# Products behind attention outputs as four products of 32 columns, one kind of PSUM bank, early identity products and another order of work, in a kernel of two transformer blocks

## The chip, the cores and the metric

The kernel runs on one core of a Trainium2 chip. The metric is the device time of one execution in microseconds, the median of several runs. "PE" is TensorE's matmul side, "PEld" its weight loads, DVE is VectorE, ACT ScalarE, POOL GpSimd, SP the engine that issues the DMAs.

## The reference

Two transformer blocks are applied to x, of 32 sequences with 128 positions and 256 features, all in fp32. Each block has self attention (16 heads of 16 features), cross attention to a context of 32 x 128 x 256, and a feed-forward layer of 1024. Both are conditioned by a vector for each sequence. Cut to what matters:

```python
# first block
mod = silu(t_emb) @ ada_w + ada_b              # six parts: shift, scale, gate for two places
xm1 = ln(x) * (1 + scale_sa) + shift_sa
q, k, v = split(xm1 @ qkv_w + qkv_b)
x = x + gate_sa * (softmax(q k^T * SCALE) v @ sa_proj_w + sa_proj_b)
qc = ln(x) @ q_w + q_b ; kc, vc = split(context @ kv_w + kv_b)
x = x + softmax(masked(qc kc^T * SCALE)) vc @ ca_proj_w + ca_proj_b
h = gelu((ln(x) * (1 + scale_ff) + shift_ff) @ fc1_w + fc1_b)
x = x + gate_ff * (h @ fc2_w + fc2_b)
# second block: the same stages, rotary embedding of q and k, adaptive layer norms before
# each stage, no gates and no biases in attention
```

## The kernel before

The 32 sequences are taken in 16 groups of two (256 columns). Each group passes through both blocks, and eight groups ("streams") are under way at a time. A stage of a stream is a Python generator. It yields when its next step could run (a time, an engine, the buffers it needs, a rank), and `Tasks.run` (L143) always steps the task that could start first on its engine. The instructions are issued in this order, and every engine executes its own in order.

The times by which it chooses are a planner's: `Clock` (L41) holds for each engine when it will be free, with costs written by hand (`clock.use("pe", 0.86 * n)`), an addition of `TURN` where PE's way of dividing its array changes ("full", "rows", "columns"), and a time for each buffer. `ORDER` (L35) holds a number for each 40 us of planned time; it changes the ranks and the patience of the choice in that stretch, and so the order of the work. None of these numbers exists at run time; only the order does.

PE divides its array in three ways. *Full*: the projections with 128 x 128 weights and 256 columns of data, that is `rows_T` (L590, products transposed to features x positions, at L598), `values` (L603, at L610) and `project` (L813, at L836), and the transposes against the identity (L559 for normalized y, L748 for the attention maxima). *Rows*: scores, 16 products of 32 rows a batch, four beside each other (`group_rows` L720, at L723). *Columns*: attention outputs, 16 products of 32 columns a batch (L769), four beside each other.

An attention batch takes: first scores (L732), the maxima by VectorE (L735, two reductions), the maxima turned by PE (L748), subtraction from the queries (L752), second scores (L757), exp by ScalarE (L761, two of them), outputs with the sums of the exponentials (L769), a copy to `ou` (L775). When both batches of a group are copied, `over_sums` (L780) sends the sums through DMAs: `few`, reciprocal, `inv` in DRAM, and back spread out as `ou`, multiplied into `xt` (L803). `project` multiplies xt by the output weights.

PSUM has eight banks: `scores` takes four (one buffer), `small` one (turned maxima and outputs, L236), `products` three (everything else, L237). A piece of PE's work takes a free one with `clock.take` and another engine's step gives it back.

At the start SP issues loads in this order: rows (L284), embT (L287), cols (L290), ada_w's first part into the place of w_fc1 (L313), x of group 0 (L317), w_qkv. PE's first products are the modulations (L448, ada_w by the silu of the condition).

Of the kernel before, what the change touches and what calls it, by code (L numbers as in the profile page):

```python
# [17 lines left out]
P = 128  # L18
# [3 lines left out]
GB = 2  # L22
# [12 lines left out]
ORDER = (  # L35
    200, 7, 0, 0, 0, 0, 297, 0, 0, 0, 0, 0, 0, 0, 0, 0, 129, 264, 0, 0, 0, 312, 0, 0, 0, 388, 0, 0, 109, 188, 182,
    0, 0, 0, 292, 58
)


class Clock:  # L41
# [3 lines left out]
    HOP, DRAIN, TABLE, PACE = 0.06, 0.22, 1.28, 1.03  # L45
    TURN = {"full": 0.15, "rows": 0.1, "columns": 0.1}

    def __init__(self):
        self.free = dict.fromkeys(("pe", "dve", "act", "pool", "sp", "none"), 0.0)
        many = {"sc": 1, "at": 1, "mm": 3, "pt": 2, "set": NA, "qa": 2, "ou": 3, "st": 2, "ht": 1,  # L50
                "y": 3, "cx": 3, "x": NS + 1}
        self.slots = {kind: [0.0] * n for kind, n in many.items()}
        self.table, self.way = None, "full"
        self.now = 0.0
        self.landed = 2.0

    def use(self, engine, took, way="full"):

        if engine in ("exp", "gelu"):
            if engine != self.table:  # L60
                took += self.TABLE
                self.table = engine
            engine = "act"
        if engine == "pe":
            took = took * self.PACE + (self.TURN[way] if way != self.way else 0.0)
            self.way = way
        self.free[engine] = max(self.now, self.free[engine]) + took
        return self.free[engine] + (self.DRAIN if engine == "pe" else self.HOP)
# [154 lines left out]
def two_blocks(ctx: ExitStack, tc: tile.TileContext, a: dict, out: bass.AP):  # L223
# [11 lines left out]
    scs = [psum.tile([P, R, C * S], F32, name="scores")]  # L235
    ats = [psum.tile([P, C * S], F32, name="small")]  # L236
    mms = [psum.tile([P, 2 * GT], F32, name=f"products{i}") for i in range(3)]  # L237
    streams = [Stream(const, i) for i in range(NS)]
# [9 lines left out]
    p_a = pool("p_a", 1)  # L248
    p_s = pool("p_s", NS + 2)

    def mm(shape):
# [10 lines left out]
    def weight(rows, cols, uses, *names):  # L262

        t = const.tile([P, rows // P, cols], F32, name=f"w_{names[0]}")

        def second():
            n = cols // len(names)
            for i, name in enumerate(names):
                load(t[:, :, i * n:(i + 1) * n], f"L1_xcond_{name}")
                end = clock.dma(6.0)  # L270
            return end

        return Weight(t, uses, second)
# [7 lines left out]
    w_fc2 = weight(DF, D, 1, "ffn_w2")  # L281

    rows = const.tile([P, C + 2], F32, name="rows")
    nc.sync.dma_start(out=rows, in_=a["rows"])  # L284

    embT = {name: const.tile([P, KC, B], F32, name=f"embT_{name}") for name in ("raw", "silu")}
    nc.sync.dma_start(out=embT["raw"], in_=a["cond_1024"])  # L287

    cols = const.tile([P, a["vectors"].shape[1]], F32, name="cols")
    nc.sync.dma_start(out=cols, in_=a["vectors"])  # L290
    for _ in range(3):
        clock.load(32)
# [12 lines left out]


    ada_lo, late = w_fc1.t, w_fc2.t.rearrange("p (k n) d -> p k (n d)", k=KC)
    ada_hi = late[:, :, 0:2 * D]
    lnw = [late[:, :, 2 * D:], ada_lo[:, :, 0:2 * D], ada_hi]
    spare = [t.rearrange("p f n -> p (f n)") for t in ht]  # L310
    clock.slots["ht"] = [NEVER]
    src = a["L0_xcond_ada_w"].rearrange("(c p) n -> p c n", p=P)
    nc.sync.dma_start(out=ada_lo[:, :, 0:2 * D], in_=src[:, :, 0:2 * D])  # L313
    t_ada = clock.load(512)

    def load_x(t, src, g):
        nc.sync.dma_start(out=t, in_=src[g * GB:(g + 1) * GB].rearrange("b s d -> s b d"))  # L317

    def load_ctx(i, g):
        nc.sync.dma_start(out=cxs[i], in_=a["ctx_1024"].rearrange("(c p) n -> p c n", p=P)[:, :, g * GT:(g + 1) * GT])  # L320

    load_x(xs[0], a["x"], 0)
    t_x0 = clock.load(256)
    load(w_qkv.t, "L0_xcond_qkv_w")
    w_qkv.there[0] = clock.load(768)

    ident = const.tile([P, P], F32, name="ident")
    make_identity(nc, ident)
    neg_half = const.tile([P, GB], F32, name="neg_half")
    nc.gpsimd.memset(neg_half, -0.5)  # L330
# [130 lines left out]
    def the_first():  # L461
        t = max(t_ada, 6.5)
        scale = yield from modulation(t, 0, "sa_scale", ada_lo, "silu", c_ada, D, D, True)
        shift = yield from modulation(t, 0, "sa_shift", ada_lo, "silu", c_ada, 0, 0, False)
        mods["L0", "sa"] = scale, shift
# [124 lines left out]
    def rows_T(w, col, src, n):  # L590
# [4 lines left out]
        for c in range(n):  # L595
            for k in range(KC):
                at = col + c * P
                nc.tensor.matmul(ps[:, c, :], lhsT=w.t[:, k, at:at + P], rhs=src[:, k, :],  # L598
                                 start=(k == 0), stop=(k == KC - 1))
        w.used()  # L600
        return slot, ps, clock.use("pe", 0.86 * n)

    def values(wm, hd, w, col, src, t):  # L603
# [4 lines left out]
        for b in range(GB):  # L608
            for k in range(KC):
                nc.tensor.matmul(ps[:, b, :], lhsT=src[:, k, b * S:(b + 1) * S],  # L610
                                 rhs=w.t[:, k, col:col + D], start=(k == 0), stop=(k == KC - 1))
        w.used()
        t = clock.use("pe", 1.72)
        there = Event()
# [49 lines left out]
    def plain(to, wm, w, src, t, bias):  # L664
# [6 lines left out]
        def move():  # L671
# [6 lines left out]
            for e in range(2):  # L678
                nc.sync.dma_start(out=to[0:P:2, e:C:2, :], in_=st[64 * e:64 * e + 64, 0:KC, :])
                end = clock.dma(2.4)  # L680
            clock.give("st", at, there.add(end))
# [4 lines left out]
    def turned(to, wm, w, col, src, t):  # L686
# [7 lines left out]
        def move():  # L694
# [10 lines left out]
            for e in range(2):  # L705
                nc.sync.dma_start(out=to[2 * e:P:4, :, :], in_=st[:, 0, e, :])
                end = clock.dma(2.4)
            clock.give("st", at, there.add(end))
# [4 lines left out]
    def attention(wm, hd, masked, t, t_v, name, done):  # L713
# [13 lines left out]
        def batch(b):  # L727
# [14 lines left out]
            clock.give("sc", slot, t_top)  # L742
            yield (lambda: max(t_top, when(second[b - 1]) if b else 0.0)), "pe", "at qa" if ou else "at qa ou", 0.5
            at, less = clock.take("at"), clock.take("qa")
            if not ou:
                ou.append(clock.take("ou"))
            ps = ats[at][:, 0:S]
            nc.tensor.transpose(ps, top.rearrange("p r i -> p (r i)"), ident)  # L748
# [4 lines left out]
            end = clock.use("dve", 0.7)  # L753
            clock.give("at", at, end)
            yield end, "pe", "sc pt", 0
# [7 lines left out]
            clock.give("sc", slot, end)  # L763
            yield (lambda: max(end, when(t_v))), "pe", "at", 1
            at = clock.take("at")
            for c in range(C):
                for r in range(R):
                    i = (R * c + r) * HD
                    nc.tensor.matmul(ats[at][32 * r:32 * r + 32, c * S:(c + 1) * S],  # L769
                                     lhsT=v[:, b, i:i + HD, :].rearrange("p d t -> p (d t)"),  # L770
# [3 lines left out]
            yield end, "act", "", 1  # L774
            nc.scalar.copy(ous[ou[0]][:, :, cut], ats[at].rearrange("p (c s) -> p c s", s=S))  # L775
            end = clock.use("act", 0.6)
            clock.give("at", at, end)
            copied.add(end)

        def over_sums():  # L780
# [6 lines left out]
            nc.sync.dma_start(out=few, in_=o[1:P:8, :, :])  # L787
            at = clock.dma(2.2)
            nc.sync.dma_start(out=wm.xt, in_=o[0:P:2, :, :])
            clock.dma(2.0)  # L790
            yield at, "dve", "", 1
# [3 lines left out]
            nc.sync.dma_start(out=inv.rearrange("r (t w) -> (r t) w", w=w), in_=few)  # L795
            yield clock.dma(1.7), "sp", "", 1
            by = o[:, 0:KC, :]
            for c in range(2):
                half = inv[:, c * KC * GT:(c + 1) * KC * GT]
                nc.sync.dma_start(out=by[c:P:2, :, :], in_=half.unsqueeze(1).to_broadcast([n, 4, KC * GT]))  # L800
                at = clock.dma(2.2)
            yield at, "dve", "", 1.5
# [10 lines left out]
    def project(wm, x, lhs, n, w, ready, bias, gate, name):  # L813


        if bias is not None:
            bias = biases[bias]
        if gate is not None:
            y, gate = gate, ys[gate]
        if bias is not None:  # L820
            for b in range(GB):
                if gate is None:
                    nc.gpsimd.tensor_tensor(x[:, b, :], x[:, b, :], bias, ALU.add)
                else:
                    gb = p_s.tile([P, D], F32, tag="gb", name=f"gb_{name}_{b}", bufs=2)
                    nc.gpsimd.tensor_tensor(gb, gate[:, b, :], bias, ALU.mult)
                    nc.gpsimd.tensor_tensor(x[:, b, :], x[:, b, :], gb, ALU.add)
                    clock.use("pool", 0.7)
                clock.use("pool", 0.7)
        for b in range(GB):  # L830
# [4 lines left out]
            for k in range(n):  # L835
                nc.tensor.matmul(ps[:, b, :], lhsT=lhs(k, b), rhs=w.t[:, k, :], start=(k == 0), stop=(k == n - 1))  # L836
            t = clock.use("pe", 0.43 * n)
        w.used()
# [55 lines left out]
    class Context:  # L894
# [5 lines left out]
        def fetch(self, wm):  # L900
# [3 lines left out]
            load_ctx(self.slot, self.g)  # L904
            self.there.add(clock.dma(3.3))

# [68 lines left out]
    def stream(wm, mine, loaded):  # L975

        while loaded:
# [13 lines left out]
            def next_x(i):  # L991
                load_x(xs[i], a["x"] if then < NG else middle, then % NG)
                return xs[i], clock.dma(3.3)

# [113 lines left out]
```

## Time and profile before

| what | value |
|---|---|
| median of 6 runs | 1481.52 us (1479.39 to 1486.67) |
| the profiled execution's own time | 1482.65 us |
| its span, first to last instruction | 1480.5 us |
| mean granted TensorE clock | 0.995 |
| PE busy, records | 1438.1 us (97%), 16992 |
| L598 on w_ffn_w, 1024 records of 128 x 256 | 238.5 us busy, mean 384 ns |
| L769 outputs, 4096 records of 128 x 128 | 138.6 us busy, mean 276 ns |
| L735 reductions of scores, 256 | 299.9 us busy, mean 1213 ns |
| L761 exp, 256 | 248.3 us busy, mean 1022 ns |
| DMA | 120.49 MB, 25.5% of 16 engines |

[...] In a timeline line the columns are the start, the length from the first start to the last end, engine, line, operation, what is written and read, the part of the array (rows*columns), the data's shape and the number of records. In brackets stands an idle time before it and what ended it. In the list of waits a line says who waited for whom: us in total, times, longest.

### The profile page before, as it was taken

The page shows a single profiled execution, that of the slowest core. Times are in us where ns is not written, and L with a number is a line of the kernel's source. Part 1 is how long each engine was busy: PE and PEld are TensorE (multiplying, and loading weights), DVE is VectorE, ACT ScalarE, POOL GpSimd, SP SyncE. Part 2 cuts the span into 40 slices and gives each one's busy share as a digit, 9 for nine tenths or more (in the row PEclk, how much of TensorE's full clock was granted, in tenths as well). Part 3 has the DMA queues.
Part 4 walks back from the last instruction along what each step waited for, and adds up shares of the span by engine and source line. Part 5 has one row for each costly group of instructions (what it writes and reads, how often), then busy time and mean ns, then how long its engine had stood idle before and what let it go on. Part 6 is the DMA issues. An engine that isn't in the chain of part 4 may idle for free.

```text
span 1480.5 us, 39505 instructions
## 1 busy us (share of the span) xinstructions
PE 1438.1 (97%) x16992; PEld 1184.1 (80%) x16992; DVE 876.5 (59%) x1514; ACT 711.7 (48%) x1150; POOL 360.3 (24%) x498
## 2 busy tenths in 40 slices
PE   7999999999999999999999999999999999999998
PEld 6787878788888887887787887888788787888887
DVE  7665555555555555557468565667487656656531
ACT  6544545445555554544444534544444443544452
POOL 3031323321232322333223231222032121202110
PEclk9999999999999999999999999999999999999999
DMA  6333223222223133233223241221223111211201
GB/s 220 123 98 91 70 61 101 69 80 84 65 78 102 57 93 97 67 94 99 68 82 105 73 140 64 65 79 55 80 83 115 64 56 57 80 41 65 73 26 40
DMA packets 107358, 120.49 MB, mean 81 GB/s; under 512 B 11632, under 2 KB 82992, under 8 KB 107184
## 3 DMA queue, kind: packets, MB, share of 16 engines
q1 hardware_dynamic: 107184, 117.98, 25.5%
q8 instruction: 133, 2.18, 0.6%
q14 instruction: 41, 0.34, 0.1%
HBM read 54.92 MB, written 12.68 MB: 46 GB/s over the span
## 4 chain that ended last, share of the span: by engine, by line
PE 79%; DMA 7%; DVE 7%; issue 2%; SPq 2%; ACT 2%; POOL 1%; DVEq 0%; ACTq 0%; POOLq 0%
PE products L598 25%; PE products L836 21%; PE scores L723 15%; PE small L769 7%; PE products L610 6%; PE products L559 3%; DVE top L735 2%; PE small L748 1%; DMA ou<-inv_a 1%; ACT exp L761 1%; DVE y L547 1%; DVE xt L803 1%; DMA ou<-inv_b 1%; DMA ou<-inv_e 1%; DMA inv_b<-few_b 1%
## 5 line engine op out<-in xcount | busy, mean ns | idle before, releaser
L761 ACT ACTIVATE exp<-scores 128x1024 f32<-128x1024 f32 x256 | 248.3, 1022 | 169.8 <-PE scores L723 160.0
L735 DVE TENSOR_REDUCE top<-scores 128x8 f32<-128x1024 f32 x256 | 299.9, 1213 | 45.1 <-PE scores L723 44.6
L598 PE MATMUL products<-xt,w_ffn_w 128*128 128x256 f32 x1024 | 238.5, 384 | 0.4 <-ACT ht L865 0.4
L836 PE MATMUL products<-w_ffn_w,ht 128*128 128x256 f32 x1024 | 232.6, 382 | 0.0
L598 PEld LDWEIGHTS products<-xt,w_ffn_w 128*128 128x128 f32 x1024 | 189.5, 190 | 31.9 <-issue 3.4
L836 PEld LDWEIGHTS products<-w_ffn_w,ht 128*128 128x128 f32 x1024 | 191.8, 190 | 28.1 <-issue 1.2
L723 PEld LDWEIGHTS scores<-qa,keys 32*128 32x128 f32 x4096 | 126.7, 187 | 51.0 <-issue 24.7
L775 ACT COPY ou<-small 128x512 f32<-128x512 f32 x128 | 75.6, 590 | 189.2 <-PE small L769 187.5
L865 ACT ACTIVATE ht<-products,cols 128x256 f32<-128x256 f32 x256 | 116.2, 474 | 104.6 <-PE products L598 103.7
L723 PE MATMUL scores<-qa,keys 32*128 32x128 f32 x4096 | 151.1, 284 | 9.1 <-ACT exp L761 3.5
L723 PEld LDWEIGHTS scores<-keys,queries 32*128 32x128 f32 x4096 | 126.0, 186 | 37.3 <-issue 22.9
L723 PE MATMUL scores<-keys,queries 32*128 32x128 f32 x4096 | 150.5, 283 | 3.3 <-ACT exp L761 1.5
L769 PE MATMUL small<-exp,values 128*32 128x128 f32 x4096 | 138.6, 276 | 2.5 <-DVE qa L752 2.4
L703 POOL TENSOR_TENSOR st<-st 128x512 f32<-128x512 f32 x64 | 83.8, 1312 | 230.0 <-DVE st L698 208.9
L841 DVE TENSOR_TENSOR x<-products,x 128x512 f32<-128x512 f32 x64 | 44.1, 688 | 139.9 <-PE products L836 139.2
L752 DVE TENSOR_TENSOR qa<-queries,small 128x512 f32<-128x512 f32 x128 | 86.9, 679 | 67.4 <-PE small L748 64.7
L598 PE MATMUL products<-xt,w_qkv_w 128*128 128x256 f32 x512 | 125.8, 392 | 0.8 <-DVE xt L579 0.8
L769 PEld LDWEIGHTS small<-exp,values 128*32 128x32 f32 x4096 | 104.2, 110 | 25.4 <-issue 11.5
L598 PEld LDWEIGHTS products<-xt,w_qkv_w 128*128 128x128 f32 x512 | 96.5, 196 | 16.5 <-issue 2.0
L803 DVE TENSOR_TENSOR xt<-xt,ou 128x512 f32<-128x512 f32 x64 | 47.8, 747 | 84.9 <-DMA ou<-inv_b 26.6
L698 DVE TENSOR_TENSOR st<-products,rope 128x512 f32<-128x512 f32 x128 | 81.5, 682 | 13.8 <-PE products L598 9.6
L845 DVE TENSOR_TENSOR y<-products,y 128x512 f32<-128x512 f32 x32 | 22.1, 690 | 109.3 <-PE products L836 93.4
(109 smaller groups left out, 1758.7 us busy)
## 6 DMA issues: line engine op xcount, KB each, us to landing
xt<-ou SPq DMA_DIRECT2D x64, 256.0 KB
keys<-st SPq DMA_DIRECT2D x96, 128.0 KB
queries<-st SPq DMA_DIRECT2D x96, 128.0 KB
cxt<-in_ctx SPq DMA_DIRECT2D x32, 256.0 KB
x<-in_x SPq DMA_DIRECT2D x16, 256.0 KB
keys<-st SPq DMA_DIRECT2D x16, 256.0 KB
y<-gate_dram_sa SPq DMA_DIRECT2D x16, 256.0 KB
ou<-inv_a SPq DMA_DIRECT2D x32, 128.0 KB
```

The source lines that it names most:

```text
L598: nc.tensor.matmul(ps[:, c, :], lhsT=w.t[:, k, at:at + P], rhs=src[:, k, :], start=(k == 0), stop=(k == KC - 1))
L610: nc.tensor.matmul(ps[:, b, :], lhsT=src[:, k, b * S:(b + 1) * S], rhs=w.t[:, k, col:col + D], start=(k == 0), stop=(k == KC - 1))
L698: nc.vector.tensor_tensor(st[:, :, :, one], ps[:, :, one].unsqueeze(2).to_broadcast([P, 2, 2, S]), rope, ALU.mult)
L703: nc.gpsimd.tensor_tensor(st[:, 0], st[:, 0], st[:, 1], ALU.add)
L723: nc.tensor.matmul(sc[:, r, c * S:(c + 1) * S], lhsT=lhs(slice(32 * r, 32 * r + 32), c), rhs=rhs(slice(32 * r, 32 * r + 32), c), start=Tru ...
L735: nc.vector.tensor_reduce(top[:, r:r + 2, TOP:TOP + 2 * C:2], scs[slot][:, r:r + 2, :].rearrange("p r (c s) -> p r c s", s=S), AX.X, ALU.max)
L752: nc.vector.tensor_tensor(qa, q[:, :, cut], ps.unsqueeze(1).to_broadcast([P, C, S]), ALU.subtract)
L761: nc.scalar.activation(exps[pt][r // 2], scs[slot][:, r:r + 2, :], AF.Exp, scale=SCALE)
L769: nc.tensor.matmul(ats[at][32 * r:32 * r + 32, c * S:(c + 1) * S], lhsT=v[:, b, i:i + HD, :].rearrange("p d t -> p (d t)"), rhs=exps[pt][r ...
L775: nc.scalar.copy(ous[ou[0]][:, :, cut], ats[at].rearrange("p (c s) -> p c s", s=S))
L836: nc.tensor.matmul(ps[:, b, :], lhsT=lhs(k, b), rhs=w.t[:, k, :], start=(k == 0), stop=(k == n - 1))
L865: nc.scalar.activation(ht[f // (FC // 2)][:, f % (FC // 2), :], ps[:, 0, :], AF.Gelu, bias=b1[:, f:f + 1])
```

## The change

Five things change:

- `multiply` replaces the plain matmul in `rows_T`, `values` and `project`. If the planner's state of PE is "columns" when the product is issued, it is issued as four products of 32 of its output rows each; otherwise as before. The planner's way "any" stays in columns if PE is there and is full otherwise. `TURN` is now charged for the way that is left.
- `small` is gone. There are four `products` banks, and turned maxima and outputs take one of these too.
- At the start embT and ada_w are loaded first, then rows, x of group 0 and cols. Twelve products of the identity with itself are issued on PE as soon as the identity is made; nothing reads them.
- `project` waits in the planner until its bias row exists.
- Some planned costs (DMA times, the time of the first modulation) and the numbers in `ORDER` are others. The order of the work differs throughout.

```diff
 ORDER = (
-    200, 7, 0, 0, 0, 0, 297, 0, 0, 0, 0, 0, 0, 0, 0, 0, 129, 264, 0, 0, 0, 312, 0, 0, 0, 388, 0, 0, 109, 188, 182,
-    0, 0, 0, 292, 58
+    76461, 23488, 0, 0, 0, 11198, 21064, 0, 0, 70525, 0, 0, 82594, 39864, 78145, 0, 87173, 36332, 67761, 88325, 0,
+    384, 0, 49384, 42794, 64772, 95724, 36861, 38189, 70264, 536, 60140, 7381, 59045, 89734, 0, 0
 )
...
-    TURN = {"full": 0.15, "rows": 0.1, "columns": 0.1}
+    TURN = {"full": 0.1, "rows": 0.15, "columns": 0.15}
...
-        many = {"sc": 1, "at": 1, "mm": 3, "pt": 2, "set": NA, "qa": 2, "ou": 3, "st": 2, "ht": 1,
+        many = {"sc": 1, "mm": 4, "pt": 2, "set": NA, "qa": 2, "ou": 3, "st": 2, "ht": 1,
...
-            took = took * self.PACE + (self.TURN[way] if way != self.way else 0.0)
+            if way == "any":
+                way = "columns" if self.way == "columns" else "full"
+            took = took * self.PACE + (self.TURN[self.way] if way != self.way else 0.0)
...
-    ats = [psum.tile([P, C * S], F32, name="small")]
-    mms = [psum.tile([P, 2 * GT], F32, name=f"products{i}") for i in range(3)]
+    mms = [psum.tile([P, 2 * GT], F32, name=f"products{i}") for i in range(4)]
...
+    def multiply(to, lhs, rhs, start=True, stop=True):
+
+        if clock.way == "columns":
+            for j in range(0, P, 32):
+                nc.tensor.matmul(to[j:j + 32], lhsT=lhs[:, j:j + 32], rhs=rhs, start=start, stop=stop)
+        else:
+            nc.tensor.matmul(to, lhsT=lhs, rhs=rhs, start=start, stop=stop)
...
+    for _ in range(12):
+        nc.tensor.matmul(mms[0][:, 0:P], lhsT=ident, rhs=ident, start=True, stop=True)
...
-                nc.tensor.matmul(ps[:, c, :], lhsT=w.t[:, k, at:at + P], rhs=src[:, k, :],
-                                 start=(k == 0), stop=(k == KC - 1))
+                multiply(ps[:, c, :], w.t[:, k, at:at + P], src[:, k, :], k == 0, k == KC - 1)
         w.used()
-        return slot, ps, clock.use("pe", 0.86 * n)
+        return slot, ps, clock.use("pe", 0.86 * n, "any")
...
-            at, less = clock.take("at"), clock.take("qa")
+            at, less = clock.take("mm"), clock.take("qa")
...
-            at = clock.take("at")
+            at = clock.take("mm")
...
-            bias = biases[bias]
+            if bias not in biases:
+                yield (lambda: 0.0 if bias in biases else NEVER), "none", "", 0
+            row = biases[bias]
...
-                nc.tensor.matmul(ps[:, b, :], lhsT=lhs(k, b), rhs=w.t[:, k, :], start=(k == 0), stop=(k == n - 1))
-            t = clock.use("pe", 0.43 * n)
+                multiply(ps[:, b, :], lhs(k, b), w.t[:, k, :], k == 0, k == n - 1)
+            t = clock.use("pe", 0.43 * n, "any")
```

## The prediction

> **What bounds the kernel now.** I read the page's head first, then the chain of work that ended last, then the timeline of TensorE (PE) alone.
>
> ```profile
> span 1480.5 us, 39505 instructions
> PE 1438.1 (97%) x16992; PEld 1184.1 (80%) x16992; DVE 876.5 (59%) x1514; ACT 711.7 (48%) x1150; POOL 360.3 (24%) x498
> ...
> PE 79%; DMA 7%; DVE 7%; issue 2%; SPq 2%; ACT 2%; POOL 1%; DVEq 0%; ACTq 0%; POOLq 0%
> ```
>
> PE is busy 97% of the span and makes 79% of the chain; VectorE and ScalarE have 40% and 50% of their time free. So the time is PE's stream, plus what PE loses between pieces, plus its waits. A busy PE is not a PE at its peak, so I split it. An fp32 product leaves two records (a transpose one). Start to start, records of 256 columns follow in 215.8 ns; of 128 columns in 109.5. Four products of 32 columns (the outputs) start within 20 ns of each other and the next four come 109.5 later; the four-row scores do it in 112. With these steps all 16992 records take 1293.9 us. PE's records reach from 5.99 to 1476.2, which is 1470.2 us. The rest, 176 us, sits where the array changes its division, and in waits. The timeline of PE shows the first kind:
>
> ```profile
> 507.69 1.17 PE L723 MATMUL scores<-qa,keys 32*128 32x128 f32 x32
> 508.79 3.72 PE L836 MATMUL products<-w_ffn_w,ht 128*128 128x256 f32 x16
> 512.44 1.08 PE L769 MATMUL small<-exp,values 128*32 128x128 f32 x32
> 513.45 1.99 PE L836 MATMUL products<-w_sa_out_w,xt 128*128 128x256 f32 x8
> 515.38 1.17 PE L723 MATMUL scores<-keys,queries 32*128 32x128 f32 x32
> ```
>
> From scores to scores 7.69 us pass. The steps make 8 x 0.112 + 16 x 0.2158 + 8 x 0.1095 + 8 x 0.2158 = 6.95. The other 0.74, with no wait, is four changes: rows to full, full to columns, columns to full, full to rows. Taken over all pieces of the trace (last start to last start, less the steps), the medians hardly scatter: into scores 0.212 from anywhere; into outputs 0.135 from full and 0.130 from rows; into full products 0.198 from columns and 0.192 from rows; into transposes of y 0.148 from columns, 0.143 from rows; into transposes of the maxima 0.089 from rows. Full behind full costs 0.00 to 0.06.
>
> **Changes of the array.** The instruction lists of both kernels give how often each happens. 474 of the 2048 large products become four of 32 columns; the scores, outputs and transposes stay.
>
> Into scores: 256 to 255, -0.2 us. Into outputs: 51 and 79 to 39 and 77, -1.9. Into full products from columns: 91 to 3, 88 x 0.198 = -17.4. From rows: 93 to 114, +4.0. Into transposes from columns: 14 to 56, 42 x 0.148 = +6.2 (for the maxima this price is y's; the one such place before was in a wait). Maxima from rows: 53 to 33, -1.8. Sum -11.1 us: a third of what is saved behind outputs comes back, since a stay in columns only moves the change to a later transpose or product.
>
> **The split products themselves.** 474 x 2 = 948 steps of four records, with a price the trace does not show for four tiles of 256 columns. The nearest rows: the single 32-column product of 256 (L472) steps at 216 ns, and outputs run four tiles at 109.5 for 128 columns, the same as a full product of 128. The 110 ns load of L769 hides in that short step. From below, 215.8 is the stream itself, so no gain; from above, the scores' 112 against 109.5 would be 5 ns a step, +5 us. I take 0, the outputs' row. PE's queue gets 1422 more product instructions, at four records in 216 ns, half the rate that outputs already show. A columns piece behind a columns piece (165 places) isn't in the trace; full behind full prices it at 0 to 0.058, so 0 to +10; I take 0, products behind products.
> [...]
>
> **The head.**
>
> ```profile
> 5.99 3.60 PE L448 MATMUL products<-embT_silu,w_ffn_w 128*128 128x32 f32 x16 [5.99 <-DMA w_ffn_w<-in_L_xcond_ada_w]
> 10.41 1.23 PE L559 MATMUL products<-ident,y 128*128 128x128 f32 x4 [0.83 <-DVE y L547]
> 12.46 6.73 PE L598 MATMUL products<-xt,w_qkv_w 128*128 128x256 f32 x16 [0.82 <-DVE xt L579]
> ...
> 23.18 1.89 PE L598 MATMUL products<-xt,w_qkv_w 128*128 128x256 f32 x8
> ```
>
> The 16 records at 12.46 step at 427 ns, later ones at 216: the array runs at half rate until 18.8, though the page's PEclk says 9. The first products of ada_w wait for its DMA (6.0). The change issues embT and ada_w first (SP 0.9 us sooner) and puts 12 identity products in the wait; the identity is ready at 1.29, and at half rate they take 24 x 0.213 = 5.1 us, to 6.5, so they cost at most 0.5 us. If the rate has doubled by 10 us, ada_w's 16 records fall from 3.4 to 1.8 and the 16 at 12.46 from 6.8 to 3.45 us. Against this, rows and cols are issued later, behind the 512 KB, and ScalarE's ten copies of 1.04 us (L353, waiting for rows) end about 1.5 us later, at 14.4, before it can evict the first keys. VectorE's first instruction (L334) waits for cols, ahead of x0's statistics, so these start little before 6.5, and y, the transposes and xt (2.1 us from 10.41 to 12.46) remain. The products then start at 11.9 and end at 15.3 instead of 19.2; keys are evicted by 18 and their DMA lands by 21. I put the first scores at 21 instead of 25.00: -4 us. From both sides: +0.5 if the rate doesn't double, -5.9 if all 5.0 us of halved steps and ada_w's 0.9 go.
> The row shows the rate doubling after 6.4 us of unbroken products. [...]
>
> **The banks and the order.** Of the 55 us beyond steps and changes, 5 are the half rate. PE's own waits are small and many:
>
> ```profile
> PE products L836 <- DVE xt L803: 6.1, 10, 2.0
> PE products L559 <- DVE y L547: 6.1, 6, 2.4
> PE products L448 <- DMA w_ffn_w<-in_L_xcond_ada_w: 6.0, 1, 6.0
> PE scores L723 <- ACT exp L761: 5.0, 7, 1.4
> PE scores L723 <- DVE top L735: 3.2, 6, 1.2
> ```
>
> To compare orders I counted, in both lists, where PE's work between a producer and its consumer is shorter than the short end (3rd percentile) of that distance in the trace: first scores to next scores or to the maxima 3.04 us, second scores to next scores 2.38, to outputs 3.49, outputs to their projection 10.67 (the DMA round through inv), projection to y's transposes 4.94, those to products 1.77, a bank of transposed maxima 1.66. Before, what is missing sums to 25 us between head and tail, 1 in the tail. After: 13 in the body (the bank's own 2.5 us are gone, with four banks taken in turn), but the last 45 us are tight. There a first scores of head 2 is followed at once by second scores (2.9 missing), then the projection of xt6 (0.5 left of 3.5), outputs right behind second scores (2.4), products behind transposes (1.7, twice) and the projection of xt5 (1.4 left of 3.1): 10.4 together. So -12 + 9.4, -2.4 us. The count sees no queueing on VectorE and ScalarE, which made the other 24 us of waits; I leave those as they are. The bounds of this whole term: -12 (the body alone) to +12 (the tail, and the saving eaten by queues).
> SP's issues in the body change places but not number; the planner's constants cost nothing at run time. What hides all this is PE's own work; if VectorE ran late, the scores' single buffer would show it first.
>
> **Sum.** 1480.5 lies in an execution of 1482.65 (2.1 around the span), against a median of 1481.52. 1482.65 - 11.1 - 4.0 - 2.4 = 1465 us.
>
> **Rivals.**
> Slower: the split products lose their overlap. Place: the 948 steps. If the 110 ns load of L769 is exposed at each, +104, 1569; 18 us gone needs 19 ns a step, so from 235 instead of 216 ns it is slower. For it: no row has four accumulating tiles of 256 columns. Against: eight outputs steps in a row at 109.5 with the same load. Chance 0.10, 1483 to 1570.
> The order eats the gain: the tail and queues on VectorE add 12 where I have -2.4, 1479; up to 1486. For it: VectorE's 1213 ns reductions sit in every chain, and tight places of outputs behind second scores rise from 7 to 13, of maxima behind first scores from 3 to 15. Chance 0.14, 1474 to 1487.
> The waits fall further, as any free bank serves any piece: -12, and the head -5.9, 1454. For it: 7.7 us of waits are at transposes, 20 at products. Chance 0.14, 1443 to 1456.
> It doesn't do what it says: the split depends on the planner's state at issue, but the list shows 151 pieces of it, each behind outputs or another; only the heating may fail: 1469, within the forecast.
> Forecast, 0.62: 1456 to 1474.
>
> **Numbers.** About 0.3% (4.4 us) is what a measurement of this kernel can tell from no change, so faster means below 1477. Forecast, falling waits and a third of the eaten gain: 0.80 faster. 0.10 within, 0.10 slower. The range reaches 1448 to 1482.
>
> **What would show it.** Split pieces stepping at 216 ns for four records (1.73 us for 32 records) and starting right behind outputs; 0.198 gaps gone behind outputs; the first qkv products at half their 6.7 us and first scores near 21; less PE idle before L836 and L559 in the body and some 9 us more in the last 45. Wrong, if the split step is above 225 ns, or PE's waits on VectorE grow in the body.

## The result, and the profile after

The changed kernel took 1485.05 us (median of 25 runs, 1479.77 to 1490.75) against 1480.67 us of the kernel before (52 runs, 1476.20 to 1486.86): ratio 1.003, 95% interval 1.0021 to 1.0039. It is slower by a little, where 1465 was forecast. The profiled execution took 1487.22 us, at a mean granted clock of 0.986 (before: 0.995). The head of its page and its chain of work that ended last:

```profile
span 1485.4 us, 45301 instructions
PE 1436.0 (97%) x19860; PEld 1140.5 (77%) x19860; DVE 876.1 (59%) x1518; ACT 714.7 (48%) x1150; POOL 358.8 (24%) x498
...
PE 76%; DMA 9%; DVE 8%; SPq 2%; issue 2%; POOL 2%; ACT 1%; DVEq 0%; POOLq 0%; ACTq 0%
```

PE's busy share is the same 97%, yet DMA and DVE have 17% of the chain where they had 14%. The timeline of PE shows that the split products do what they are meant to do:

```profile
492.47 1.08 PE L783 MATMUL products<-exp,values 128*32 128x128 f32 x32
493.37 1.91 PE L256 MATMUL products<-w_sa_out_w,xt 128*32 128x256 f32 x32
495.21 1.17 PE L737 MATMUL scores<-qa,keys 32*128 32x128 f32 x32
```

The outputs need 8 steps of 0.1095 = 0.88 us, and the split products (L256) start 0.90 after them: the 0.198 behind outputs is gone. Their 32 records take 8 steps of 0.216. The list of PE's waits, which had its longest (but for the first load) at 2.4 us, now reads:

```profile
PE products L258 <- DVE xt L817: 11.4, 10, 2.4
PE products L575 <- DVE y L563: 7.6, 9, 2.5
PE products L256 <- DVE xt L817: 7.5, 2, 6.5
PE scores L737 <- DVE top L749: 5.9, 7, 2.5
PE products L258 <- DMA w_qkv_w<-in_L_xcond_qkv_w: 3.2, 1, 3.2
```

The projections (L256 and L258, waiting for xt) stood for 18.9 us instead of 6.1. I split the time of PE in each profiled execution as the prediction did: steps, changes of the array (its medians times their number), and what is left, which is waits and steps at half rate. That rest is given for the first 25 us, the last 45 us, and between ("body").

| profiled execution | steps | changes | head | body | last 45 us |
|---|---|---|---|---|---|
| before | 1293.9 | 121.2 | 7.1 | 46.8 | 1.0 |
| after (12 identity products: 2.6 of the steps) | 1296.5 | 109.9 | 6.8 | 55.9 | 8.9 |
| forecast for the difference | 0 | -11.1 | -4.0 | -12 | +9.4 |
| measured difference | +2.6 | -11.3 | -0.3 | +9.1 | +7.9 |

(The first record starts at 1.3 instead of 6.0. The identity products fill that place: 2.6 us of steps, and 2.1 us of half rate that the row leaves out.) Two of the four forecasts came true, the head gave nothing, and the body went the other way by 21 us. About 5 of the body's 9.1 us are steps at half rate, the rest are waits: before has three stretches at a granted clock of 0.50 there (from 131.2, 267.8 and 728.6; 13.6 us long together), after has four (from 79.0, 102.9, 577.3 and 826.5; 27.2 us).

### The profile page after: what moved, and what is told of

Read it like the earlier page. It is cut to its first block, busy times and chain, and to the rows that moved or that the text cites. A ratio compares the mean times of both kernels' runs of the same rounds, so it can differ in the third digit from the quotient of the medians.

```text
span 1485.4 us, 45301 instructions
## 1 busy us (share of the span) xinstructions
PE 1436.0 (97%) x19860; PEld 1140.5 (77%) x19860; DVE 876.1 (59%) x1518; ACT 714.7 (48%) x1150; POOL 358.8 (24%) x498
## 4 chain that ended last, share of the span: by engine, by line
PE 76%; DMA 9%; DVE 8%; SPq 2%; issue 2%; POOL 2%; ACT 1%; DVEq 0%; POOLq 0%; ACTq 0%
PE products L258 39%; PE scores L737 15%; PE products L256 10%; PE products L783 7%; DVE top L749 3%; PE products L575 3%; PE products L762 1%; DMA ou<-inv_e 1%; DMA inv_a<-few_a 1%; DMA ou<-inv_a 1%; DMA ou<-inv_d 1%; SPq L814 1%; DVE y L563 1%; DVE st L712 1%; DVE xt L817 1%
## 5 line engine op out<-in xcount | busy, mean ns | idle before, releaser
L258 PE MATMUL products<-xt,w_ffn_w 128*128 128x256 f32 x780 | 181.6, 384 | 1.8 <-ACT xt L593 1.8
L258 PE MATMUL products<-w_ffn_w,ht 128*128 128x256 f32 x800 | 183.0, 382 | 0.0
L258 PEld LDWEIGHTS products<-w_ffn_w,ht 128*128 128x128 f32 x800 | 149.4, 190 | 22.0
L258 PEld LDWEIGHTS products<-xt,w_ffn_w 128*128 128x128 f32 x780 | 144.0, 190 | 25.0 <-ACT xt L593 3.2
L789 ACT COPY ou<-products 128x512 f32<-128x512 f32 x128 | 75.3, 589 | 155.4 <-PE products L783 155.2
L783 PE MATMUL products<-exp,values 128*32 128x128 f32 x4096 | 137.5, 276 | 0.7 <-ACT exp L775 0.7
L766 DVE TENSOR_TENSOR qa<-queries,products 128x512 f32<-128x512 f32 x128 | 86.1, 675 | 66.1 <-PE products L762 63.7
L783 PEld LDWEIGHTS products<-exp,values 128*32 128x32 f32 x4096 | 105.6, 110 | 21.6 <-issue 9.3
L258 PE MATMUL products<-xt,w_qkv_w 128*128 128x256 f32 x400 | 99.9, 396 | 4.0 <-DMA w_qkv_w<-in_L_xcond_qkv_w 3.2
L632 ACT COPY values<-products 128x512 f32<-128x512 f32 x64 | 40.6, 634 | 112.1 <-PE products L258 93.5
L258 PEld LDWEIGHTS products<-xt,w_qkv_w 128*128 128x128 f32 x400 | 75.8, 197 | 16.2 <-DMA w_qkv_w<-in_L_xcond_qkv_w 3.3
```

Of the source, the lines that this page charges most:

```text
L258: nc.tensor.matmul(to, lhsT=lhs, rhs=rhs, start=start, stop=stop)
L766: nc.vector.tensor_tensor(qa, q[:, :, cut], ps.unsqueeze(1).to_broadcast([P, C, S]), ALU.subtract)
L783: nc.tensor.matmul(mms[at][32 * r:32 * r + 32, c * S:(c + 1) * S], lhsT=v[:, b, i:i + HD, :].rearrange("p d t -> p (d t)"), rhs=exps[pt][r ...
L789: nc.scalar.copy(ous[ou[0]][:, :, cut], mms[at].rearrange("p (c s) -> p c s", s=S))
```

## The experiments

Theory, from here on: **PE is paced by the DMA rounds of the sums.** VectorE, whose records follow the order of issue, stands at the reciprocal of few and at xt until the DMAs land (125 us in before's profile), and PE's projections, and its scores behind the reductions that are queued there, end their waits on it (xt 18.9 and `top` 5.9 us in the changed kernel's list above). What PE saves, it then waits. To this comes the clock: behind a stand PE runs at half rate for 3.4 us or more (the changed kernel's four stretches at a granted clock of 0.50 above last 3.4 to 10.2 us). Rivals: the split products cost something that steps don't show; the new order is bad by itself; the waits are VectorE's and ScalarE's own work.

**e1: the split alone, in before's order.** Every product keeps its place; `multiply` looks at the way of the product issued last.

```diff
+        if now["way"] == "columns":
+            for j in range(0, P, 32):
+                nc.tensor.matmul(to[j:j + 32], lhsT=lhs[:, j:j + 32], rhs=rhs, start=start, stop=stop)
```

> The kernel before with its order of work and its banks untouched; only, a large product that is issued while the array is in columns is issued as four products of 32 columns (618 of 2048 products). Theory (the split is worth what the changes of the array cost, 0.198 us behind outputs, and the order ate it): the changes cost 121.2 us before and 108.1 here by the medians of the trace, so 13 us less, near 1467, ratio 0.991; some of it may turn into waits, so 0.990 to 0.995. Rival (the split products bring a cost that the steps don't show, which made the changed kernel slower): 1480 or more.

Measured: 1488.33 us against 1482.27, ratio 1.0033 (1.0016 to 1.0051). My theory missed. Changes fell from 121.2 to 108.1 us, and the body's rest rose by 17.4, from 46.8 to 64.2: as much as the 13.1 that were saved, 3.2 more of steps at half rate (8.5 against 5.3), and 1 us besides. (The profiled execution, 1485.23, lies 3 us under e1's median.) One place in both timelines, first of before, then of e1; in brackets stands the idle time and what ended it:

```profile
1061.03 1.17 PE L723 MATMUL scores<-qa,keys 32*128 32x128 f32 x32 [1.15 <-DVE top L735]
1062.14 3.72 PE L836 MATMUL products<-w_ffn_w,ht 128*128 128x256 f32 x16
```
```profile
1066.79 1.17 PE L736 MATMUL scores<-qa,keys 32*128 32x128 f32 x32 [3.37 <-DVE top L749]
1067.89 5.41 PE L260 MATMUL products<-w_ffn_w,ht 128*128 128x256 f32 x16
```

The same scores wait 3.37 instead of 1.15 us, and the same 16 records behind them take 5.41 instead of 3.72. VectorE's timeline tells why the reductions (`top`) came late: before, then e1:

```profile
1058.02 0.69 DVE L803 TENSOR_TENSOR xt<-xt,ou 128x512 f32<-128x512 f32 x1 [2.12 <-DMA ou<-inv_d]
1058.63 2.35 DVE L735 TENSOR_REDUCE top<-scores 128x8 f32<-128x1024 f32 x2
```
```profile
1063.77 0.69 DVE L819 TENSOR_TENSOR xt<-xt,ou 128x512 f32<-128x512 f32 x1 [3.41 <-DMA ou<-inv_d]
1064.38 2.35 DVE L749 TENSOR_REDUCE top<-scores 128x8 f32<-128x1024 f32 x2
```

VectorE stands at xt for a DMA, and the reduction that PE needs is behind it. Over the whole execution VectorE waits 125 us for DMAs of the rounds (few and xt) in before and 155.5 us in e1. (In the changed kernel it is 131 us; there the rounds show in PE's waits for xt, 18.9 us above.) The stretches around that stand in e1 give the clock (columns: stretch, its length, busy time and records of PE, PEld, DVE, ACT and POOL, granted clock, DMA share, GB/s):

```profile
1064.40:1067.90 3.50, 1.11 (x33) 0.99 (x33) 2.33 (x3) 0.00 (x0) 0.00 (x0) 1.00 0.00 0
1067.90:1071.30 3.40, 3.40 (x12) 2.77 (x9) 0.00 (x0) 3.22 (x3) 0.00 (x0) 0.51 0.00 0
1071.30:1074.70 3.40, 3.40 (x57) 2.66 (x60) 0.69 (x1) 0.33 (x1) 0.00 (x0) 0.99 0.00 0
```

**e2: e1 with the four banks taken in turn.** The same order; only the bank that a piece gets is another.

```diff
+    empty, held = [0, 1, 2, 3], {}
...
+        if kind in ("mm", "at"):
+            held[kind, i] = empty.pop(0)
...
+            empty.append(held.pop((kind, i)))
```

> As the first, and the four banks outside of scores are one kind, taken in turn; the order of work stays that of before. Theory: the waits for the one small bank were counted as 2.5 us, so up to 3 us under the first kernel, 1464 to 1467. Rival (shared banks make products wait behind outputs or maxima): 3 us or more above the first kernel.

Measured: 1481.45, ratio 0.9991 (0.9974 to 1.0009). The level forecast was missed again, and the banks are worth 0.4% where I had counted 2.5 us; the body's rest is 54.5. With the banks in turn the split costs nothing, but it gains nothing either.

**e3: the changed kernel without the split.**

```diff
-        if clock.way == "columns":
+        if False:
```

> The changed kernel in its own order of work, with every large product whole. Theory: changes of the array cost 109.9 us in the changed kernel and 120.2 here, so 10 us more, 1495, ratio to the kernel before 1.010. Rival (the split itself costs): at or under 1485.

Measured: 1490.80, ratio 1.0057 (1.0037 to 1.0077). In after's order the split gives 0.27%, 4 us of the 10.3 by which the changes differ (120.2 against 109.9); the intervals just touch. So it is the rest of the change that is slower: order, banks, loads and identity products without the split are 0.57% above before.

**e4: the changed kernel without the identity products.**

```diff
-    for _ in range(12):
+    for _ in range(0):
```

> The changed kernel without its twelve identity products. Theory (the rate had fallen back by the first large products, at 10.8 us, so the twelve products gave nothing): the modulations run at half rate from 5 to 8.5 us and end when they did, so the time is that of the changed kernel within 1.5 us, 1485. Rival (they are worth what was forecast): 1488 or more.

Measured: 1487.91, ratio 1.0033 (1.0014 to 1.0051), as the changed kernel's 1.003: the twelve products are worth nothing that shows (each interval reaches 0.1 to 0.2% to either side).

**e5 and e6: the round left out, without and with the split.** Both keep PE's list of products, product for product: e5 that of before, e6 that of e1.

```diff
-            nc.sync.dma_start(out=few, in_=o[1:P:8, :, :])
...
-            nc.vector.reciprocal(few, few)
...
-            nc.sync.dma_start(out=inv.rearrange("r (t w) -> (r t) w", w=w), in_=few)
...
-                nc.sync.dma_start(out=by[c:P:2, :, :], in_=half.unsqueeze(1).to_broadcast([n, 4, KC * GT]))
...
-            nc.vector.tensor_tensor(wm.xt, wm.xt, by, ALU.mult)
+            nc.vector.tensor_tensor(wm.xt, wm.xt, wm.xt, ALU.max)
```

> The kernel before with the DMA round of the sums left out: few, its reciprocal, inv and the copy back to ou are gone, and xt is only copied by VectorE, so the attention outputs are not divided by their sums. PE's list of products is that of before. Theory (the round stands in VectorE's queue in front of the reductions and ends PE's waits): VectorE's waits on DMA, 129 us in before, fall below 60, PE's waits beyond steps and changes fall from 55 to about 35 us, time about 1462. Rival (PE's waits come from VectorE's and ScalarE's own work): within 5 us of before, 1477 or more.

> e1 (before's order, products behind outputs split) with the same round left out as in e5, so the outputs are not divided here either. The array changes save 13.1 us of PE's time against e5. Theory (e1 gained nothing because PE only came earlier to the end of a DMA round, and longer stands halved the clock): with the round gone the saving shows, 10 to 14 us under e5, about 1450. Rival (the split itself slows something that the steps don't show): no gain over e5 here either, within 5 us of it or above, as e1 was 6 us above before.

Measured, against 1481.85: e5 1460.74, ratio 0.9860 (0.9839 to 0.9880); e6 1450.54, ratio 0.9792 (0.9769 to 0.9815). This is the pair that decides. With the round, the split cost 6 us; without it, the same split saves 10.2 us of the 13.1 by which the changes fall. The heads of the two pages, e5 first:

```profile
span 1459.5 us, 38966 instructions
PE 1429.9 (98%) x16992; PEld 1180.9 (81%) x16992; DVE 821.7 (56%) x1450; ACT 711.5 (49%) x1150; POOL 361.9 (25%) x498
```
```profile
span 1447.2 us, 46390 instructions
PE 1414.0 (98%) x20700; PEld 1107.9 (77%) x20700; DVE 823.2 (57%) x1450; ACT 711.8 (49%) x1150; POOL 362.3 (25%) x498
```

PE's rest is 34.0 us in e5, as expected, and VectorE's waits for DMAs are below 15 us in both. The body's rest is 26.5 in e5 and 28.1 in e6, so PE no longer waits away what it saves, and the split costs nothing by itself. The half rate goes with the round: the granted clock is 0.999 in e5 and 1.000 in e6, and by it no stretch of e6's body ran at half rate. What the pair doesn't tell apart is which part of the round paces PE: its DMAs, or the 54 us of VectorE's work (876 to 822) that went with them in both.

**e11: the changed kernel with the round left out** (the edit of e5).

> The changed kernel with the round of the sums left out as in e5 and e6, so the outputs are not divided. Theory (its body lost to the rounds and the clock behind the stands, not to its order as such): PE's waits fall from 72 to about 40 us, the stand at 824 is gone, time about 1455, under e5's 1461. Rival (its tight places of PE, VectorE and ScalarE cost by themselves): 1465 or more, above e5.

Measured: 1449.30, ratio 0.9777 (0.9763 to 0.9791).

```profile
span 1446.5 us, 44743 instructions
...
PE 91%; DVE 4%; DMA 2%; POOL 1%; issue 1%; ACT 1%; SPq 0%; DVEq 0%; ACTq 0%; POOLq 0%
```

PE is now 91% of the chain and DMA 2%. Its body's rest is 18.4 against 26.5 in e5, which is -8.1; its last 45 us hold 8.6 as in the changed kernel. So the new order is better than the old one in the body, as forecast, when no round is waited for. As a whole it is not: e6 has before's order and the split, and 0.9792 against e11's 0.9777 is no difference by the intervals. What e11 gains in the body (18.4 against 28.1) it gives back in its last 45 us and in the identity products. The round costs 1481.85 - 1460.74 = 21 us in before and 1485.05 - 1449.30 = 36 us after (medians of different series of runs).

**e7: ten more identity products in the head**, five ahead of the first transposes, five ahead of the first qkv products, in the changed kernel.

```diff
+        for _ in range(keep.pop("transposes", 0)):
+            nc.tensor.matmul(mms[slot][:, 0:P], lhsT=ident, rhs=ident, start=True, stop=True)
...
+        for _ in range(keep.pop("products", 0)):
+            nc.tensor.matmul(mms[slot][:, 0:P], lhsT=ident, rhs=ident, start=True, stop=True)
```

> The changed kernel with five more products of the identity ahead of the first transposes and five ahead of the first qkv products. Theory (the clock fell at 10.7 because PE stood between the first small pieces): no half rate from 10 to 18 us, the first 16 qkv records take about 3.5 us instead of 6.77, first scores about 22 instead of 24.6, 2 to 3 us under the changed kernel. Rival (the first scores wait for ScalarE's copies, not for the products): qkv faster but first scores within 0.7 us of 24.6, no gain.

Measured: 1480.43 against 1481.85, ratio 1.0000 (0.9983 to 1.0018): 0.30% under the changed kernel, 4 us, where 2 to 3 were forecast. The head's rest is 1.4 instead of 6.8. The changed kernel's head, then e7's:

```profile
1.34 5.49 PE L344 MATMUL products<-ident 128*128 128x128 f32 x24 [1.34 <-POOL ident masks.py:199]
6.62 2.20 PE L464 MATMUL products<-embT_silu,w_ffn_w 128*128 128x32 f32 x16
9.65 0.87 PE L575 MATMUL products<-ident,y 128*128 128x128 f32 x4 [0.82 <-DVE y L563]
11.35 6.77 PE L258 MATMUL products<-xt,w_qkv_w 128*128 128x256 f32 x16 [0.82 <-DVE xt L595]
...
24.60 1.17 PE L737 MATMUL scores<-keys,queries 32*128 32x128 f32 x32 [0.98 <-DMA keys<-st]
```
```profile
7.58 1.36 PE L575 MATMUL products<-ident 128*128 128x128 f32 x10
9.03 0.87 PE L578 MATMUL products<-ident,y 128*128 128x128 f32 x4
9.74 1.28 PE L615 MATMUL products<-ident 128*128 128x128 f32 x10
10.86 3.80 PE L259 MATMUL products<-xt,w_qkv_w 128*128 128x256 f32 x16
...
20.73 1.17 PE L742 MATMUL scores<-keys,queries 32*128 32x128 f32 x32
```

Behind the twelve identity products the rate rose (the records at 6.62 step at 0.21 us and from 7.35 on at 0.11; in before all 16 of this form step at 0.21). Behind two stands of 0.82 us between small pieces it fell again (granted clock 0.50 from 10.7 on), and the 16 records take 6.77 us. With the two gaps filled they take 3.80, and the first scores start at 20.73: where the prediction had put them. All eight profiles with identity products agree: the four with the ten products (e7, e9, e10, e12) have no half-rate stretch in the rest of the head, the four with the twelve alone (the changed kernel, e3, e8, e11) have one from 8.5 to 11.6 us on.

**e8: identity products in three long stands of the changed kernel** (near 103.6, 576.3 and 830.8). The place ahead of the projections:

```diff
+                for _ in range(fill.pop(name, 0)):
+                    multiply(mms[slot][:, 0:P], ident, ident)
```

> The changed kernel with products of the identity put into its three long stands: 11 ahead of the projection near 103.6, 28 (as four of 32 columns) ahead of the one at 830.8, 14 ahead of the values at 576.3. Nothing reads them. Theory (a long stand of PE halves the clock in the stretch behind it): the half-rate stretches at 102.9, 577.3 and 826.5 are gone, 6 us less in steps, 4 to 6 us under the changed kernel. Rival (the clock falls for another reason, or the fill delays what follows): the stretches stay or move, within 2 us of the changed kernel or above it.

Measured: 1485.17 in ten of twelve executions (the other two took 5004 and 6887 us, for a reason that stays open), ratio 1.0024 (1.0010 to 1.0038). Half true: the half-rate stretches at 102.9 and 577.3, which the profiles of e4 and e7 have too, are gone, that at 826.5 is 3.4 us long instead of 10.2, and steps at half rate cost some 6 us less (7.7 instead of 13.9). But the fills are 11.6 us of steps, other stands grew, three new stretches of 3.4 us came (from 141, 339 and 1015), and the time stayed. The stretch at 79.0 is gone as well, where nothing was filled, so one profile is weak evidence on a single stretch. The filler fits the theory of the stands, and it buys nothing in the middle of the kernel.

**e9: e2 with the identity products in the head** (12 and five and five, as in e7).

> e2 (before's order and loads, split products, banks in turn) with 12 products of the identity at the start, five ahead of the first transposes and five ahead of the first qkv products. Theory (PE kept busy keeps the full clock, as in e7): first qkv records at half their 6.7 us, first scores 3 us sooner than in e2, 3 to 4 us under e2's ratio of 0.9991: about 1478, ratio 0.997. Rival (in this order the first scores wait for the later loads and ScalarE's copies): within 1.5 us of e2's ratio.

Measured: 1474.50 (1465.14 to 1479.94) against 1481.62, ratio 0.9940 (0.9914 to 0.9965). That is below before, and the changed kernel stood at 1.003: the best of the versions. First scores start at 22.15 instead of e2's 24.41, so 2.3 us are the head's. Why the median is 7 under e2's stays open. The profiled execution is a poor witness: in e9's seven the time falls as the granted clock rises, from 1479.94 us at 0.991 to 1465.14 at 0.997, and the profiled one has 0.993. The clock alone isn't it, as e2 took 1476.62 at 0.997.

**e10 and e12: xt multiplied by GpSimd**, in e9 and in e7, so that VectorE's reductions aren't behind the second half of the round (the reciprocal of few stays on VectorE).

```diff
-            nc.vector.tensor_tensor(wm.xt, wm.xt, by, ALU.mult)
+            nc.gpsimd.tensor_tensor(wm.xt, wm.xt, by, ALU.mult)
```

> e9 with the product of xt and the spread sums issued on GpSimd instead of VectorE; nothing else is moved. Theory (VectorE standing at xt for the DMA round holds up the reductions behind it): PE's waits for top (7.8 us in e2) fall below 3, those for xt grow by 0.6 us each as GpSimd takes about 1.3 us where VectorE took 0.69; 4 to 8 us under e9, about 1472. Rival (the round only moves to GpSimd's queue, where rstd stands behind it): PE's waits for y grow from 7 to 15 or more, no gain over e9 or slower.

> e7 (the changed kernel with ten more products of the identity) with the product of xt and the spread sums on GpSimd. Theory, as for e10: 4 to 8 us under e7's 1480.4, about 1474, PE's waits for top below 3 us. Rival, as for e10: PE's waits for y grow past 12 us, time as e7 or above.

Measured, against 1481.62: e10 1481.39, ratio 0.9996 (0.9983 to 1.0009); e12 1503.35, ratio 1.0143 (1.0128 to 1.0157). No gain, as the rivals had it, but not for their reason. PE's waits in e9, then in e10:

```profile
PE products L284 <- DVE xt L851: 11.7, 12, 2.3
PE products L604 <- DVE y L589: 6.5, 6, 3.2
...
PE scores L768 <- DVE top L781: 5.0, 9, 1.1
PE products L281 <- DVE xt L851: 3.0, 4, 1.2
```
```profile
PE products L284 <- POOL xt L851: 17.6, 11, 6.1
PE products L604 <- DVE y L589: 6.4, 7, 3.3
...
PE products L281 <- POOL xt L851: 4.8, 5, 1.6
PE scores L768 <- DVE top L781: 1.8, 5, 0.5
```

The scores wait 3.2 us less for `top`, as the theory had it, and y is as before, against the rival. But the projections wait 7.7 us more for xt. GpSimd took 1.27 us for a tensor_tensor of this size (128 x 512, `x<-y,x` in e2's profile) where VectorE took 0.69 for xt, which over these 16 waits can make 9 us, so the 7.7 need no other cause. Shown is that the place of xt in VectorE's queue is worth about 3 us of PE's waits; what the rest of the round costs by itself, the pair doesn't tell. In e12 `top` stays (5.5 to 5.6 us) and the waits for xt double, from 18.7 to 38.0.

## Why the prediction was wrong, step by step

**Changes of the array: right.** -11.3 us against -11.1. The split products' step, 0 extra, held, and a columns piece behind a columns piece starts with no gap (0.000, median). The slower rival (a step above 235 ns) did not come: the step stayed at 216.

**From saved changes to saved time: wrong.** The sum took all 11.1 us off the time, as if PE's own stream set the end at each place. e1 and e6 show the condition: the saving is 10.2 us where no round is waited for, and below nothing where one is (nothing with the banks in turn, e2; 4 us in the new order, e3). The prediction's own sign of being wrong came: PE's waits on VectorE's xt grew from 6.1 to 18.9 us.

**Head, -4.0: wrong.** The step that failed is "If the rate has doubled by 10 us": it had doubled by 7.35 (the records at 6.62 step at 0.21 and from there on at 0.11) and was halved again from 10.7 to 17.5, as the granted clock shows. First the changed kernel, then e7 in the same stretch (columns as above):

```profile
1.00:7.30 6.30, 5.96 (x28) 5.96 (x29) 0.96 (x4) 3.38 (x5) 5.64 (x13) 1.00 0.78 251
7.30:10.70 3.40, 2.40 (x18) 1.86 (x17) 1.93 (x9) 3.40 (x4) 0.92 (x2) 1.00 0.97 324
10.70:17.50 6.80, 6.15 (x15) 4.85 (x16) 4.83 (x17) 5.77 (x9) 1.84 (x4) 0.50 0.75 256
```
```profile
10.70:17.50 6.80, 6.56 (x35) 5.34 (x34) 5.40 (x18) 6.80 (x13) 1.84 (x4) 1.00 0.77 255
```

The bound from above (+0.5) held, and e7 shows that the chain behind the products was costed rightly.

**Body, -12: wrong, measured +9.1, and the largest error.** The step that failed is the price "outputs to their projection 10.67 (the DMA round through inv)", the short end of that distance. In the twelve places where PE waited for xt in the changed kernel, 10 to 17 us passed from the outputs to the projection, over 13 in six of them, and a count against the shortest finds no wait there. The second thing the term lacked is the clock: it has half rate only in the head, though before's body already lost about 5 us to it. The worst round, from the changed kernel's SP timeline, VectorE's and PE's:

```profile
812.64 0.38 SPq L270 DMA_DIRECT2D w_ffn_w<-in_L_xcond_ffn_w  x1
...
814.30 0.56 SPq L801 DMA_DIRECT2D few_d<-ou  x1
...
822.24 0.38 SPq L270 DMA_DIRECT2D w_ffn_w<-in_L_xcond_ffn_w  x1
822.72 1.18 SPq L814 DMA_DIRECT2D ou<-inv_d  x2
```
```profile
819.79 0.95 DVE L806 RECIPROCAL few_d<-few_d 128x128 f32<-128x128 f32 x1 [4.59 <-DMA few_d<-ou]
...
830.05 0.69 DVE L817 TENSOR_TENSOR xt<-xt,ou 128x512 f32<-128x512 f32 x1 [7.06 <-DMA ou<-inv_d]
```
```profile
830.79 3.64 PE L256 MATMUL products<-w_sa_out_w,xt 128*32 128x256 f32 x32 [6.48 <-DVE xt L817]
```

From the issue of few to the projection's start (830.79) 16.5 us pass, with a weight load of the second block issued ahead of each of the two waited-for transfers; PE stands 6.48 us and then runs at half rate. The transfer behind the second weight load lands after 7.0 us; the other 23 of few and ou whose landing this trace shows took at most 4.0. That points at the weight loads for this one place, but no run here moved them, and what lengthens the other rounds stays open. That the rounds as a whole, with their work on VectorE, are the cause is shown: without them the body goes by -8.1 us (e11 against e5), near the -12 of the count. The order's numbers alone, without the other edits, were not tried.

**Last 45 us, +9.4: right** (+7.9), and 8.6 of it stays without the round: these are the short distances of scores, as counted.

**The bounds.** The whole term of banks and order was bounded by -12 and +12; body and tail together came to +17. The bound had no room for a wait with half rate behind it (6.48 us ahead of 830.79, and a granted clock of 0.50 from 826.5 to 836.8). The rival "the order eats the gain" was the nearest in mechanism (VectorE's queue), and its 1474 to 1487 holds the measured 1485.05; it was given 0.14. (Two slips of the sum change nothing: the six distances of the last 45 us add to 10.6 as printed, not 10.4, and -12 + 9.4 is -2.6.)

## What to carry to other kernels

A change that shortens the busiest engine is worth its size only where that engine's waits don't end on a chain that the change leaves as long as it was; before summing up what it saves, ask at each wait whether the releaser moves too. To try that cheaply, leave the chain out in both versions and compare: here the same edit cost 6 us with the DMA round and saved 10 without. Price a round through DMA queues at what it takes when it is waited for, not at its shortest, and add to a long stand the steps at half rate behind it (here 1.2 to 1.5 us for each 3.4 us of half rate, behind 48 of 59 stands of 2 us or more).

## What the runs showed of the hardware that I had not expected

**Half rate behind short stands.** Over the 14 profiled executions (head and end left out), a stand of PE of over 2.5 us was followed within 3.6 us by a stretch at half the granted clock 34 times of 37, one of 2 to 2.5 us 14 times of 22, one of 1 to 2 us 13 times of 101, and a shorter one (0.15 to 1 us) 11 times of 350. A stretch lasts 3.4, 6.8 or 10.2 us and costs 1.2 to 1.5 us in steps for each 3.4. Executions of one kernel differ by it too: of e2's twelve the three longest (1486.41 to 1487.86 us) have a granted clock of 0.991 or 0.992, the two shortest (1476.06 and 1476.62) 0.995 and 0.997.

**At the start the row of the clock and the steps disagree.** The stretch from 1.0 to 7.3 us of the changed kernel reads as a granted clock of 1.00, while its 24 identity records of 128 columns step at 0.21 us, twice the later 0.11.

**Four column tiles overlapped fully here**: four records of 32 columns by 256 start within 20 ns of each other and take 216 ns a step, as long as one record of a full product (215.8); coming from them, transposes of the maxima cost a change of 0.094 us where I had taken 0.148.
